# Weight loads of a mixed attention, convolution and scan kernel put on ScalarE's queue, and the fronts of its scan branches moved to other steps

## The chip, the cores and the metric

The kernel runs on one core of a Trainium2 chip. The metric is the device time of one launch in microseconds (us). Before the change it is 6692.09 us, the median of three executions that lie between 6676.76 and 6695.76 us. The profile shown here is of one further execution, with a span of 6680.2 us.

## The reference, cut to what matters

The input is a batch of 8 images of 256 channels and 32x32 pixels (1024 tokens), in float32. Four residual layers follow each other; each adds to `x` a function of the group-normalised `x`:

```
x = x + L0(gn(x))   # attention with 8 heads of 64, q and k normalised by length
x = x + L1(gn(x))   # 3x3 convolution 256 -> 256
x = x + L2(gn(x))   # 3x3 convolution 256 -> 256
x = x + L3(gn(x))   # layer norm, 4 Mamba branches (64 channels each, state of 16),
                    # gates, 1-d convolutions, a second attention, layer norms, 3x3 depthwise
```

A Mamba branch projects its 64 channels to 128, applies a short convolution and a gate, makes a step size `dt` and the vectors `B` and `C`, and runs along the 1024 tokens the recurrence `h = exp(dt*A)*h + dt*u*B`, `y = C.h`, for each of 128x16 states.

## The kernel before, in words

**Two streams side by side.** While the scans of image b run (`scan_layers`, L1019), the dense work of its neighbours runs beside them (`dense`, L1488): the last part of layer 3 of image b-1 (`back_layers`, L1184), the first attention of image b+1 (`front_attention`, L595), and then the two convolutions of image b+1 (`front_convs`, L769) mixed with the end of image b-1 (`back_end`, L1366). `interleave` (L1438) writes the two streams into one program: each dense piece yields a cost, and a step of the scans is put in whenever the costs have added up to `PACE` (2.95 for the middle images). So the six middle images repeat the same pattern.

**The order of instructions.** The framework lays the program out ahead of the run: each engine gets a fixed list, mostly in the order in which the pieces were written, and a buffer is given out again when its last reader is done. On the chip an engine works through its own list in order and waits at any entry whose inputs or buffer are not ready. Transfers are entries of such a list too: those written `nc.sync.dma_start` stand in SyncE's list (SP in the profile), those written `nc.scalar.dma_start` would stand in ScalarE's, between its activations. Before the change all 3328 transfers of the normal path stand in SyncE's list.

**The weights.** Small weights are loaded once. The large ones go through `chunk` (L150): it takes one of six buffers of the pool `wsp` (L45), loads a piece of 128 to 256 KB, and the matmuls right after it use it. The trace has 392 such loads (L156), 49 an image: 24 of them are the pieces of the two 3x3 convolutions (`in_wc1`, `in_wc2`; 192 KB, 12 matmuls written in the kernel as 3 taps x 2 halves with two passes each in the trace), the others are for the projections (`wqk`, `wv`, `wout`, `ainqk`, `ainv`, `rpw`, `fpw`, `fcw`, `projw`).

**The other transfers.** A scan unit is a quarter of the states of one half of the tokens, in two groups; there are 64 units an image, 16 a branch. `load` (inside `scan_steps`, L904) fetches two units ahead: `bc` (L937) every second unit, `dt` and `du` (L927) at the start of each half. Each is four transfers, into pools of two or three buffers. `store` (L795, its transfers at L799) writes `dt` and `du` of a branch to DRAM, L846 the rows of B and C.

**A unit on the engines.** GpSimd multiplies du by B (L950), ScalarE makes the decays `da` (an exp into PSUM), VectorE runs the scan over `hs`, GpSimd multiplies by C (L982), TensorE adds up over the states into `y`.

**The fronts.** What a branch needs before its first unit is made by `branch_front` (L803), a generator in six pieces: 0 the input projection into `raw`; 1 the short convolution `u` (one activation, three multiply-adds on VectorE, a tanh, one more multiply-add); 2 the projection `low` of u with `w_mxpw` and the storing of B and C; 3 dt before its softplus; 4 the softplus and the storing of dt; 5 du and its storing. `fronts` (L1040) says at which count n of scan steps each next piece is due (n is two more than the unit whose decays are being made). The tile `u` has two buffers (L818), so branch i takes over that of branch i-2, which `branch_back` (L876) reads for the last time in its second piece, two steps after the last unit's `y`.

In the profile nearly all engine work has line L102, the line of a helper (`Paced`) that records every operation, so the groups are told apart by their tiles: `big<-im,w` is a 3x3 convolution, `big<-local,w` the first half of the `fcw` projection, `da<-u,w_mxpw` piece 2 of a front.

Of the kernel before, what the change touches and what calls it, by code (L numbers as in the profile page):

```python
# [33 lines left out]
def preact_stack(ctx: ExitStack, tc: tile.TileContext, I, out, cols):  # L34
# [3 lines left out]
    nc = tc.nc  # L38
# [37 lines left out]
    def mwork(name):  # L76
        return mp.tile([P, N], F32, tag="m", name=name)

    def xm_tile(name):
        return xmp.tile([P, TP], F32, tag="xm", name=name)  # L80
# [69 lines left out]
    def chunk(name, i):  # L150

        src = fc_w if name == "fcw" else I[name]
        k, n = src.shape[2:]
        t = wsp.tile([P, HALF], F32, tag="w", name="w")
        t = t[:, 0 : k * n].rearrange("p (k n) -> p k n", n=n)
        nc.sync.dma_start(out=t, in_=src[i])  # L156
        return t

    minw = resident("minw")
# [23 lines left out]
    for base, sign in ((0, 1), (7, -1)):  # L183
        nc.gpsimd.affine_select(
            out=gmat,
            in_=gmat,
# [84 lines left out]
    def group_stats(mv, psum):  # L271

        with urgent():
            pg = psum()
            tensor.matmul(
                pg[:, 0:4], gmat, mv.rearrange("p a b -> p (a b)"), start=True, stop=True
            )
            g = sp.tile([P, 2, 2], F32, tag="g", name="g", bufs=4)
            vector.tensor_copy(g.rearrange("p a b -> p (a b)"), pg[:, 0:4])
            d = sp.tile([P, 2], F32, tag="d", name="d")  # L280
            vector.tensor_sub(d, mv[:, :, 0], g[:, :, 0])
            vector.tensor_mul(d, d, d)
            pd = psum()
            tensor.matmul(pd[:, 0:2], gmat, d, start=True, stop=True)
            rs = sp.tile([P, 2], F32, tag="rs", name="rs", bufs=4)
            vector.scalar_tensor_tensor(
                rs, pd[:, 0:2], 1e-5, g[:, :, 1], ALU.add, ALU.add
            )
            inverse_root(rs)
            shift = sp.tile([P, 2], F32, tag="shift", name="shift", bufs=4)  # L290
            vector.scalar_tensor_tensor(
                shift, g[:, :, 0], -1.0, rs, ALU.mult, ALU.mult
            )
        return rs, shift

    def group_norm(xt, stats, dsts, view=lambda a: a):
        with urgent():
            scale, shift = stats
            for t in range(2):
                scalar.activation(  # L300
                    dsts[t],
                    view(xt[:, t]),
                    AF.Identity,
                    bias=shift[:, t : t + 1],
                    scale=scale[:, t : t + 1],
                )
# [59 lines left out]
    def affine(wname, bname, func=AF.Identity):  # L366
        def finish(t, part):
            scalar.activation(
                part, part, func, bias=col(bname, t), scale=col(wname, t)
            )  # L370

        return finish

    def zero_ends(t):
        vector.memset(t[:, 0:1], 0.0)
        vector.memset(t[:, N + 1 : N + 2], 0.0)

    def inner(t):
        return t[:, 1 : N + 1]
# [11 lines left out]
    def project(name, srcs, evac):  # L391

        last = len(srcs) - 1
        for m in range(2):
            w = chunk(name, m)
            ps = big_tile()
            for k, src in enumerate(srcs):
                for h in range(2):
                    tensor.matmul(
                        ps[:, HALVES[h]],  # L400
                        w[:, k],
                        src[:, HALVES[h]],
                        start=k == 0,
                        stop=k == last,
                    )
            evac(m, ps)
            yield 2 * len(srcs) * 0.86

    def project_both(name, srcs, evac):

        last = len(srcs) - 1
        w = [chunk(name, m) for m in range(2)]
        ps = [big_tile() for _ in range(2)]
        for k, src in enumerate(srcs):
            for m in range(2):
                for h in range(2):
                    tensor.matmul(
                        ps[m][:, HALVES[h]],
                        w[m][:, k],
                        src[:, HALVES[h]],  # L420
                        start=k == 0,
                        stop=k == last,
                    )
                if k == last:
                    evac(m, ps[m])
            yield 4 * 0.86
# [168 lines left out]
    def front_attention(src, img, exact=False):  # L595
# [8 lines left out]

        v = vp.tile([P, NKT, 512], F32, tag="v", name="v")
        wv = [chunk("wv", c)[:, 0] for c in range(2)]
        for kt in range(0, NKT, 2):
            ps = big_tile()
# [267 lines left out]
    def branch_back(i, xn, br):  # L876

        j, rows = i // 2, slice((i % 2) * 64, (i % 2) * 64 + 64)
        u, z = br["u"], mwork("z")
        for h in range(2):  # L880
            ps = da_tile()
            tensor.matmul(
                ps,
                minw[rows, j, P : 2 * P],
                inner(xn[j])[rows, HALVES[h]],
                start=True,
                stop=True,
            )
            zh = z[:, HALVES[h]]
            scalar.activation(zh, ps, AF.Tanh, scale=0.5)  # L890
            vector.scalar_tensor_tensor(zh, zh, 1.0, ps, ALU.add, ALU.mult)
        vector.tensor_mul(u[:, 0:N], u[:, 0:N], z[:, 0:N])
        yield
        for h in range(2):
            ps = da_tile()
            tensor.matmul(
                ps[rows], moutw[:, i], u[:, HALVES[h]], start=True, stop=True
            )
            part = inner(xn[j])[rows, HALVES[h]]
            vector.scalar_tensor_tensor(  # L900
                part, part, half_skip[rows], ps[rows], ALU.mult, ALU.add
            )
# [116 lines left out]
    def scan_layers(img):  # L1019


        xt = img.pop("x")
        img["stats"] = group_stats(img.pop("mv"), da_tile)
        xn = [xm_tile("xn0"), xm_tile("xn1")]
        for t in xn:
            zero_ends(t)
        group_norm(xt, img["stats"], [inner(t) for t in xn])
        img["xd"] = xdp.tile([P, 2, N], F32, tag="xd", name="xd")
        nc.sync.dma_start(out=img["xd"], in_=xt)
        sq = [mwork("ln_sq"), mwork("ln_sq")]  # L1030
        yield
        yield from layer_norm(
            [inner(t) for t in xn], sq, BY_HALF, da_tile, affine("norm_w", "norm_b")
        )
        yield
        branches = [{} for _ in range(NB)]
        for _ in branch_front(0, xn, branches[0]):
            yield

        def fronts():  # L1040
            for i in range(1, NB):
                for n, _ in enumerate(branch_front(i, xn, branches[i])):
                    yield 16 * i - 10 + 7 * n // 4

        front, ending, due, n = fronts(), iter(()), 0, 0
        steps = scan_steps(branches)
        while True:
            next(ending, None)
            while due is not None and n >= due:
                due = next(front, None)  # L1050
            if next(steps, END) is END:
                break
            yield
            done = next(steps)
            if done is not None:
                ending = branch_back(done, xn, branches[done])
            n += 1
            yield
        yield from ending
        img["xm"] = xn  # L1060
# [471 lines left out]
    with tc.If(again > 0):  # L1532
        with tc.For_i(0, batch, 1) as i:
            img = {}
            src = x_in[bass.ds(i, 1)].rearrange("o (t p) n -> p (o t) n", p=P)
# [113 lines left out]
```

## Time and profile before

| | busy us | share of the span | instructions |
|---|---|---|---|
| TensorE (PE) | 5489.3 | 82% | 17310 |
| VectorE (DVE) | 4001.5 | 60% | 4612 |
| GpSimd (POOL) | 2723.7 | 41% | 1302 |
| ScalarE (ACT) | 2721.9 | 41% | 3253 |
| 16 DMA engines, SyncE's queue | | 24.6% | 216408 packets |

The granted TensorE clock is 0.891 of full speed in the mean. A middle image takes 799 us (for instance 1575 to 2374 us), with TensorE busy in 673.9 of them, VectorE in 508.9, ScalarE in 340.1 and GpSimd in 341.2.

How to read it: the share of an engine says little where the stages differ, so the reading goes by waits. A line of waits names the engine that waited and the tile it was to write, then what came last before it went on, then the total, the number of waits and the longest. `SPq` is SyncE's queue: time there is a transfer that stood at the head of the list and could not be issued yet. `PEld` is the loading of weights into TensorE, which overlaps the matmuls.

### The profile page before, as it was taken

To read this page: it belongs to the slowest core of one execution; us is meant where nothing else is said; L and a number is where in the kernel's file an instruction comes from. 1 tells how busy PE (TensorE), PEld (TensorE's weight loads), DVE (VectorE), ACT (ScalarE), POOL (GpSimd) and SP (SyncE) were. 2 spreads that over 40 slices of the span, in tenths; PEclk is the share of its full clock that TensorE was granted. 3 is DMA by queue.
4 is the path that set the end of the run, shared out by engine and by line. 5 is a ranking of instruction groups with operands and counts; after the bars stand their busy time and mean duration, and the time that the engine had idled before them with its cause. 6 is when DMAs were issued, how large, how long until landed. Compare 5 with 4: busy or idle time off the path is not lost.

```text
span 6680.2 us, 52240 instructions
## 1 busy us (share of the span) xinstructions
PE 5489.3 (82%) x17310; PEld 1854.4 (28%) x17310; DVE 4001.5 (60%) x4612; ACT 2721.9 (41%) x3253; POOL 2723.7 (41%) x1302
## 2 busy tenths in 40 slices
PE   8887688896988968888698886899788896877596
PEld 2331133222322223222242222322233222321232
DVE  4247744677555775467755667557765577555532
ACT  3234424553245523544335442354424553345332
POOL 0016662534435243542526435253352534456600
PEclk9988798998989989999899998999889897988697
DMA  1022232212223122321222212232122312233300
GB/s 50 27 60 79 74 92 73 83 58 68 86 74 91 42 76 71 94 81 44 79 82 77 78 50 78 73 88 70 54 86 72 91 51 73 77 93 84 90 20 30
DMA packets 216690, 470.83 MB, mean 70 GB/s; under 512 B 60116, under 2 KB 101716, under 8 KB 214360
## 3 DMA queue, kind: packets, MB, share of 16 engines
q1 hardware_dynamic: 216408, 467.38, 24.6%
q8 instruction: 139, 2.28, 0.1%
q14 instruction: 143, 1.17, 0.1%
HBM read 394.31 MB, written 64.49 MB: 69 GB/s over the span
## 4 chain that ended last, share of the span: by engine, by line
PE 55%; DVE 25%; issue 6%; DMA 5%; ACT 5%; POOL 3%; SPq 1%; DVEq 0%; POOLq 0%; ACTq 0%
PE big L102 36%; PE acc L102 11%; DVE p L102 6%; DVE hs L102 6%; PE da L102 5%; PE y L102 3%; DVE u L102 2%; POOL hs L982 2%; DVE t L102 2%; POOL hs L950 2%; DVE dw L102 1%; DVE dt L102 1%; DMA dt<-dt_m 1%; DVE y L102 1%; DVE st L102 1%
## 5 line engine op out<-in xcount | busy, mean ns | idle before, releaser
L950 POOL TENSOR_TENSOR hs<-du,bc 128x1024 f32<-128x1024 f32 x512 | 1310.7, 2573 | 1537.3 <-DMA dt<-dt_m 1182.9
L982 POOL TENSOR_TENSOR hs<-hs,bc 128x1024 f32<-128x1024 f32 x512 | 1327.0, 2592 | 1013.3 <-DVE hs L102 951.0
L102 PE MATMUL big<-im,w 128*128 128x512 f32 x2304 | 1096.9, 630 | 338.5 <-DMA w<-in_wc 253.1
L102 ACT ACTIVATE p<-big 128x1024 f32<-128x1024 f32 x1024 | 1039.5, 1021 | 799.1 <-PE big L102 795.3
L102 PE MATMUL acc<-p,v 128*64 128x512 f32 x4096 | 1167.4, 640 | 0.7 <-ACT o L102 0.7
L102 ACT ACTIVATE da<-dt,a_neg 128x512 f32<-128x512 f32 x1024 | 687.7, 687 | 1004.7 <-DVE hs L102 711.6
L102 DVE TENSOR_TENSOR p<-p 128x1024 f32<-128x1024 f32 x448 | 777.0, 1734 | 271.4 <-ACT p L102 183.3
L102 DVE TENSOR_TENSOR_SCAN hs<-da,hs 128x512 f32<-128x512 f32 x512 | 603.0, 1210 | 477.4 <-ACT da L102 250.6
L102 DVE TENSOR_TENSOR_SCAN hs<-da,carry,hs 128x512 f32<-128x512 f32 x512 | 624.9, 1266 | 256.9 <-POOL hs L950 133.9
L102 PE MATMUL big<-qk,qk 64*128 64x512 f32 x2048 | 655.0, 674 | 105.9 <-ACT p L102 94.1
L102 PEld LDWEIGHTS big<-im,w 128*128 128x128 f32 x2304 | 447.7, 200 | 999.1 <-issue 870.3
L102 PE MATMUL big<-q,k 64*128 64x512 f32 x2048 | 604.8, 661 | 79.1 <-ACT big L102 39.6
L981 POOL COPY carry<-hs 128x2 f32<-128x2 f32 x256 | 95.8, 374 | 1089.8 <-DVE hs L102 1060.3
L102 PE MATMUL y<-hs,sel 128*32 128x512 f32 x2048 | 408.8, 723 | 153.7 <-POOL hs L982 153.5
L102 PEld LDWEIGHTS acc<-p,v 128*64 128x64 f32 x4096 | 214.1, 138 | 827.9 <-issue 732.3
L102 PEld LDWEIGHTS big<-qk,qk 64*128 64x128 f32 x2048 | 178.0, 195 | 570.9 <-issue 298.3
L102 PEld LDWEIGHTS big<-q,k 64*128 64x128 f32 x2048 | 162.8, 191 | 509.9 <-issue 274.6
L102 DVE SCALAR_TENSOR_TENSOR dw<-xo,vec,dw 128x992 f32<-128x992 f32 (+1 forms) x128 | 227.4, 1824 | 27.3 <-ACT dw L102 26.7
L102 PE MATMUL big<-xn,w 128*128 128x512 f32 x512 | 232.6, 608 | 6.7 <-ACT p L102 6.7
L102 DVE SCALAR_TENSOR_TENSOR xt<-big,vec,xt 128x1024 f32<-128x1024 f32 x48 | 61.4, 1280 | 226.9 <-PE big L102 226.9
L102 PE MATMUL big<-o,w 128*128 128x512 f32 x384 | 179.0, 615 | 15.9 <-DVE o L102 15.9
L102 DVE SCALAR_TENSOR_TENSOR u<-raw,vec,u 128x1024 f32<-128x1024 f32 x96 | 150.1, 1564 | 64.4 <-ACT u L102 63.9
(210 smaller groups left out, 4987.2 us busy)
## 6 DMA issues: line engine op xcount, KB each, us to landing
bc<-bc SPq DMA_DIRECT2D x1024, 128.0 KB
dt<-dt_m SPq DMA_DIRECT2D x512, 128.0 KB
du<-du_m SPq DMA_DIRECT2D x512, 128.0 KB
w<-in_wc SPq DMA_DIRECT2D x192, 192.0 KB
rs<-inv SPq DMA_DIRECT2D x64, 256.0 KB
dt_m<-dt SPq DMA_DIRECT2D x64, 256.0 KB
du_m<-a SPq DMA_DIRECT2D x64, 256.0 KB
xt<-in_x SPq DMA_DIRECT2D x8, 1024.0 KB
```

What stands on the lines that cost most here:

```text
L102: made = issue(*args, **kwargs)
L950: nc.gpsimd.tensor_mul(u["hs"], u["du"], both_groups(u["bc"][:, 0]))
L981: nc.gpsimd.tensor_copy(carry[:, u["q"], g : g + 2], hs[:, :, HALF - 1])
L982: nc.gpsimd.tensor_mul(hs, hs, both_groups(u["bc"][:, 1]))
```

## The change

Two edits. The loads of the weights that stay only for their use are issued from ScalarE's list in place of SyncE's. And the pieces of the fronts of branches 1 to 3 become due at other steps: the offsets from 16*i were -10, -9, -7, -5, -3, -2 and become -12, -10, -8, -6, -3, -1. The value yielded after piece k is when piece k+1 is due; that after the last piece is when piece 0 of the next branch is due. So pieces 1 to 5 of branch 1 move from n = 6, 7, 9, 11, 13 to 4, 6, 8, 10, 13, and piece 0 of branch 2 from 14 to 15.

What it is for: the weights no longer stand in one list with the transfers of the scans, and the pieces of a front lie further apart.

```diff
@@ def chunk(name, i):
         t = wsp.tile([P, HALF], F32, tag="w", name="w")
         t = t[:, 0 : k * n].rearrange("p (k n) -> p k n", n=n)
-        nc.sync.dma_start(out=t, in_=src[i])
+        nc.scalar.dma_start(out=t, in_=src[i])
         return t
@@ def scan_layers(img):
         def fronts():
             for i in range(1, NB):
                 for n, _ in enumerate(branch_front(i, xn, branches[i])):
-                    yield 16 * i - 10 + 7 * n // 4
+                    yield 16 * i - 12 + 9 * n // 4
```

## The prediction

> **What bounds the kernel now.** I read the page first, then who waited for whom, then the waits of SyncE's own queue, then the timeline of the longest wait.
>
> The chain that ended last is mostly TensorE:
>
> ```profile
> PE 55%; DVE 25%; issue 6%; DMA 5%; ACT 5%; POOL 3%; SPq 1%; DVEq 0%; POOLq 0%; ACTq 0%
> ```
>
> TensorE is busy for 5489 of 6680 us, so a time saved must come from its 1191 us of idling or shorten something it waits for. Three of its waits concern the edits:
>
> ```profile
> PE big L102 <- DMA w<-in_wc: 253.1, 8, 40.3
> ...
> PE da L102 <- DVE u L102: 80.7, 16, 8.8
> ...
> PE big L102 <- DMA w<-fc_w: 65.1, 7, 10.1
> ```
>
> The first is the prize: a convolution stands for a weight piece eight times, six of them for 39 to 40 us, once in each middle image; the other two (image 1) are 17.4 us together. Bandwidth is not why: the DMA engines are 24.6% busy. SyncE's queue, which has all transfers in one list, shows why:
>
> ```profile
> SPq L156 <- PE big L102: 1132.6, 216, 34.1
> SPq L937 <- POOL hs L982: 928.1, 130, 34.0
> ...
> SPq L927 <- ACT da L102: 504.1, 89, 21.4
> SPq L927 <- POOL hs L950: 456.8, 79, 15.2
> ```
>
> Weights (L156) stand there until TensorE frees one of six buffers, and the scans' loads (L937, L927) until the scan frees theirs. Either holds up the other. The timelines of SyncE and of TensorE in one such case (start, length, instruction, count):
>
> ```profile
> 1560.27 2.05 SPq L156 DMA_DIRECT2D w<-in_wc  x2
> 1571.11 1.73 SPq L927 DMA_DIRECT2D du<-du_m  x4
> ...
> 1638.44 1.70 SPq L927 DMA_DIRECT2D du<-du_m  x4
> 1640.18 0.88 SPq L937 DMA_DIRECT2D bc<-bc  x2
> 1651.97 11.66 SPq L927 DMA_DIRECT2D dt<-dt_m  x8
> 1663.74 1.75 SPq L927 DMA_DIRECT2D du<-du_m  x4
> 1665.59 0.37 SPq L156 DMA_DIRECT2D w<-in_wc  x1
> ```
> ```profile
> 1627.44 2.84 PE L102 MATMUL big<-im,w 128*128 128x512 f32 x6
> 1669.36 2.90 PE L102 MATMUL big<-im,w 128*128 128x512 f32 x3 [39.08 <-DMA w<-in_wc]
> ```
>
> From 1562 to 1665 us no weight is issued, while the convolution uses up its six buffers (1575 to 1630). The first of the six was free again at about 1585, when its twelve matmuls were over; the next pieces stood behind du, dt and bc of the next half, which waited for the scan. The three matmuls after the gap take 0.97 us each in place of 0.45.
>
> **What the Trainium skill says.** "DMA: Bandwidth & Descriptors", section "Anatomy of one DMA — SWDGE (gpsimd) path", says that DMA engines do not wait on semaphores: any wait happens on the issuing sequencer before dispatch. The rows of SyncE's queue agree (1132.6 us at L156). The same page, section "Issuing engines are not separate DMA queues", says that issuing from several engines only saves the sequencer's issue time, since all run on the same 16 DMA engines. So the edit buys no bandwidth; what this trace adds is that it also takes a wait at the head of one list away from the other.
>
> **The change, part by part.**
>
> *Convolution weights.* On ScalarE a piece stands between activations and can go when its buffer is free. ScalarE is busy for 9.5 us of the 39, so it gets to it long before 1665. I take the wait as gone. What comes in its place? The busy times over the stages of these convolutions:
>
> ```profile
> core 0: us, PE busy (x) PEld busy (x) DVE busy (x) ACT busy (x) POOL busy (x), PEclk, DMA share, GB/s
> ...
> 1575.00:1630.00 55.00, 51.63 (x152) 21.97 (x152) 36.41 (x44) 25.68 (x29) 29.78 (x15) 0.88 0.24 72
> 1630.00:1669.00 39.00, 0.29 (x1) 0.00 (x0) 35.16 (x33) 9.48 (x11) 17.57 (x7) 0.57 0.28 73
> 1669.00:1713.00 44.00, 40.87 (x104) 15.51 (x104) 32.39 (x25) 5.93 (x9) 30.98 (x15) 0.95 0.34 93
> 1713.00:1840.00 127.00, 112.49 (x344) 50.84 (x344) 70.65 (x113) 42.36 (x51) 49.71 (x25) 0.91 0.26 82
> ```
>
> VectorE works through the gap (35.2 of 39 us: scans and depthwise convolution) and takes the convolution's result out. If all its work of 1630 to 1713 (35.2 + 32.4 = 67.6 us) must still come before the second convolution, these 83 us shrink by only 15. If it can slide into the second convolution, where VectorE has 127 - 71 = 56 us free, all 39 are saved. I take the middle, 27 us an image.
>
> *The fc weights.* 65.1 us in seven waits, about 10 an image. The matmuls they release are followed by others on `o`, whose factors `rs` are loaded at the same time, so I count half: 5 us.
>
> *The other weights* made no wait worth naming, so moving them gains nothing; TensorE's earlier work hides them.
>
> *The fronts.* Pieces 1 and 2 of branch 1 were one step apart (n = 6, 7); now two (4, 6). In the middle images TensorE waits 8.7 us for u in the first of these places and 3.1 us in the second (11.9 an image), with the matmuls of the attention queued behind `da<-u`. A step is 7 to 12 us there (a scan unit begins every 7 to 12 us around 1940 us), so one more step could hide it; the matmul may also just be taken up sooner and wait the same. Half: 6 us. For branches 2 and 3, piece 1 is now due at n = 16i-12, in the step where branch i-2's `u` is still to be read; it waits for that buffer for about one step and then has lost its lead. No gain, no loss: the pieces after it are due a step earlier or at the same step. dt is stored a step sooner; its loads waited for dt's storing rarely (dt rows of ScalarE's waits: 61.6 us in the whole run), so nothing.
>
> *What ScalarE pays.* An issue on SyncE takes 0.36 us (median of the 192 convolution loads; 0.33 to 0.42). The skill gives about 0.05 us for dispatch in the same section "Anatomy of one DMA"; the trace decides. 49 x 0.36 = 17.6 us an image. And it adds a wait: ScalarE may reach a convolution's piece before TensorE has freed the buffer. Behind it in ScalarE's list stand the decays of the scan, for which VectorE waits, and in the attention the exps, for which TensorE waits. The trace cannot show it; the bounds are 0 and one piece of matmuls (12 in 5.35 us) for each of 24 pieces, 128 us. I take 1 us each, 24 us, since ScalarE mostly waits for VectorE and for TensorE itself there and so comes late. Of ScalarE's time few us count: it has 5% of the chain at 41% busy, one in eight. (17.6 + 24)/8 = 5 us an image.
>
> *Sum.* A middle image gains 27 + 5 + 6 - 5 = 33 us; six make 198. Image 1 with its 17.4 us of waits gains about 12, the first and last nothing. 6692 - 210 = 6482 us.
>
> **The rivals.**
> (a) *VectorE becomes the bound.* For it: 35 of 39 us busy in the gap. Then the convolution gains 10, fc 5, the fronts 0, ScalarE costs 5: 10 us x 6 = 60, so 6632 us. Against it: 56 us free in the next stage.
> (b) *All of it is recovered.* 39 + 10 + 12 - 2 = 59 us x 6 + 25 = 379: 6313 us. For it: the matmuls after a gap also run slower, which ends. Against: VectorE, as above.
> (c) *Slower: the wait moves to ScalarE.* If it meets each piece early it stands up to 128 + 18 = 146 us an image, and the decays and exps behind it stand too; if a third of it is on the path, 48 us, against 38 gained: ten us an image over eight, 80 us slower, 6772 us. For it: 216 waits at L156 for TensorE now, and the transfers share completion semaphores (rows of SyncE's waits where a load stands for an unrelated transfer, as L937, bc, for du_m<-a, 26.3 us), so ScalarE could also come to wait for SyncE's transfers. Against it: ScalarE is idle for 460 of 799 us.
> (d) *No change:* the scan sets the pace through the `y` matmuls, 6690 us.
>
> **How the numbers follow.** The forecast 0.50, (a) 0.22, (b) 0.09, (c) 0.13, (d) 0.06. The forecast is that of the likeliest, 6482. The range reaches from near (b), 6340, where about 0.07 lies below, to 6710, which takes in (a) and (d) and leaves out most of (c), about 0.12. Faster by over 0.3% (below 6672): 0.50 + 0.22 + 0.09 = 0.81; same 0.06; slower 0.13.
>
> **What would show it.** Right: `PE big <- DMA w<-in_wc` falls from 253 us to under 30 and `w<-fc_w` from 65 to under 35, a middle image takes about 766 us, TensorE's busy time stays near 5480, the rows of SyncE's queue at L156 are gone. Fronts: the 8.7 us wait for u falls. Rival (a): VectorE over 90% busy through both convolutions, TensorE's evacuations waiting for it. Rival (c): `ACT` rows that end with `PE big` at the place of the loads, longer waits of `DVE hs` for `ACT da` (372.9 us now) and of `PE big` for `ACT p` (128.1 now). I would be wrong if the pieces stood as late in ScalarE's list as in SyncE's, behind decays that wait for the scan: then TensorE's 39 us would stay.

## The result, and the profile after

The changed kernel takes 6536.18 us (median; 6529.43 to 6541.66) beside 6685.99 us for the kernel before in the same comparison (6676.76 to 6695.76). The ratio is 0.9775, with a 95% interval from 0.9756 to 0.9795: faster by 150 us. The forecast was 6482 us, a gain of 210.

Who waited for whom in the changed kernel (engine and tile, what it waited for: total us, times, longest us):

```profile
ACT da L102 <- PE big L102: 299.3, 42, 10.2
...
DVE hs L102 <- ACT da L102: 275.8, 128, 11.1
PE y L102 <- POOL hs L982: 267.9, 101, 16.0
...
PE big L102 <- ACT p L102: 180.4, 56, 13.5
...
PE da L102 <- DVE u L102: 10.0, 2, 8.4
```

The waits of TensorE for `w<-in_wc` (253.1 us before) and for `w<-fc_w` (65.1) have no row any more, and that for `u` fell from 80.7 to 10.0. In their place stand other rows: `PE y` for GpSimd grew from 153.5 to 267.9 us, `PE big` for `p` from 128.1 to 180.4. With the weights moved alone the first of these is 254.9 and the second 119.9; with the fronts moved alone they are 173.3 and 170.5, so the one comes with the weights and the other with the fronts. The row at the top is new: ScalarE waits for TensorE where its next entry is a piece of weights whose buffer is in use. What it delays most, the decays that VectorE waits for, is waited for less than before (275.8 in place of 372.9).

SyncE's queue in the changed kernel:

```profile
...
SPq L937 <- POOL hs L982: 623.8, 100, 26.6
...
SPq L927 <- POOL hs L950: 490.8, 65, 17.6
...
SPq L937 <- DMA w<-in_wc: 258.6, 39, 9.7
```

L156 is gone. The last row is a surprise: loads of `bc` on SyncE wait until a weight that ScalarE issued has landed. The weights now go out between activations (ScalarE's timeline in a middle image: start, length, instruction, count):

```profile
2336.13 0.33 ACTq L156 DMA_DIRECT2D w<-in_wc  x1
2336.51 0.69 ACT L102 ACTIVATE da<-dt,a_neg 128x512 f32<-128x512 f32 x1 [4.90 <-DVE raw L102]
...
2351.09 0.33 ACTq L156 DMA_DIRECT2D w<-in_wc  x1
...
2360.11 0.33 ACTq L156 DMA_DIRECT2D w<-in_wc  x1
...
2371.65 0.33 ACTq L156 DMA_DIRECT2D w<-in_wc  x1
```

One piece every 5 to 12 us here, where SyncE had issued none for 103 us in the passage that the prediction shows. But the convolution gave back a good part of the 39 us. Here are the busy times of the first convolution of the fourth image, and of its second with what follows, up to the first matmul of the attention's stage (`big<-rd,w`): of before, and then of after (stretch, length, then busy us of PE, PEld, DVE, ACT, POOL; TensorE clock, DMA share, GB/s):

```profile
2374.10:2521.90 147.80, 95.44 (x268) 38.29 (x268) 110.89 (x116) 42.16 (x50) 82.93 (x38) 0.80 0.29 80
2521.90:2639.10 117.20, 109.52 (x333) 49.86 (x333) 63.75 (x97) 41.45 (x50) 45.06 (x23) 0.94 0.25 81
```
```profile
2328.90:2455.70 126.80, 97.73 (x259) 38.61 (x257) 103.39 (x112) 39.41 (x47) 65.61 (x30) 0.85 0.28 80
2455.70:2578.10 122.40, 111.16 (x339) 49.57 (x337) 64.42 (x99) 40.23 (x49) 57.27 (x30) 0.95 0.29 90
```

The first stretch is 21.0 us shorter and the second 5.2 longer. VectorE is 82% busy in the first, from 75%. TensorE's own waits in that first stretch, before and after, show what came in place of the 39 us:

```profile
PE big L102 <- DMA w<-in_wc: 39.1, 1, 39.1
PE big L102 <- ACT im L102: 4.6, 1, 4.6
PE y L102 <- POOL hs L982: 3.3, 3, 1.2
...
```
```profile
PE y L102 <- POOL hs L982: 18.6, 7, 8.6
PE da L102 <- DVE t L102: 6.0, 1, 6.0
...
```

TensorE now waits for the scans' products themselves, seven times, and for VectorE. With the smaller rows its waits there fell from 50.5 us to 29.1; without the 39.1 alone they would have been 11.4.

To find the rest I cut each trace at the matmuls of stages that occur once an image: the two convolutions (`big<-im,w`), the tail between the end of the second and the first `big<-rd,w` (the start of `back_layers` and of the next scans), the stage of the attention from `big<-rd,w` to `big<-local,w`, and the rest up to the next convolution. The columns are the stages of the passage that begins with the third image's first convolution, in us, and the span of the scans that start in it. "Weights" stands for the new queue, "fronts" for the new steps.

| kernel | conv 1 | conv 2 | tail | attention | rest | image | its scans |
|---|---|---|---|---|---|---|---|
| before | 147.9 | 94.9 | 22.4 | 294.6 | 239.1 | 798.9 | 692.8 |
| after | 126.6 | 97.8 | 24.9 | 278.0 | 240.4 | 767.7 | 659.1 |
| weights alone | 132.8 | 97.9 | 25.1 | 289.6 | 240.3 | 785.6 | 680.5 |
| fronts alone | 141.6 | 95.3 | 25.7 | 278.6 | 240.5 | 781.6 | 672.5 |

And the whole span of each profiled run, cut at the first `big<-rd,w` of images 0, 6 and 7 (counted from 0, so image 1 is the second), as differences from before:

| kernel | start (1041.0) | six middle images (4793.3) | last scans (554.8) | end (291.0) |
|---|---|---|---|---|
| after | +1.3 | -174.6 | +34.8 | -1.8 |
| weights alone | +7.7 | -88.4 | +30.9 | -1.7 |
| fronts alone | -9.4 | -120.0 | +13.9 | -1.3 |

So a middle image gained 29.1 us (174.6/6; forecast 33), and the scans of the last image lost 34.8 us, which no step of the prediction had.

### The profile page after: what moved, and what is told of

Its sections match the earlier page's. It is cut to its first block, busy times and chain, and to the rows that moved or that the text cites. A ratio compares the mean times of both kernels' runs of the same rounds, so it can differ in the third digit from the quotient of the medians.

```text
span 6539.9 us, 52206 instructions
## 1 busy us (share of the span) xinstructions
PE 5511.5 (84%) x17310; PEld 1859.0 (28%) x17310; DVE 4006.1 (61%) x4612; ACT 2718.8 (42%) x3253; POOL 2704.5 (41%) x1302
## 5 line engine op out<-in xcount | busy, mean ns | idle before, releaser
L982 POOL TENSOR_TENSOR hs<-hs,bc 128x1024 f32<-128x1024 f32 x512 | 1311.3, 2562 | 952.2 <-DVE hs L102 860.5
L102 PE MATMUL acc<-p,v 128*64 128x512 f32 x4096 | 1153.3, 637 | 3.1 <-ACT p L102 1.3
L102 DVE TENSOR_TENSOR p<-p 128x1024 f32<-128x1024 f32 x448 | 766.1, 1710 | 312.1 <-ACT p L102 180.4
L102 PE MATMUL big<-qk,qk 64*128 64x512 f32 x2048 | 641.0, 671 | 142.2 <-ACT p L102 130.3
L102 PE MATMUL y<-hs,sel 128*32 128x512 f32 x2048 | 442.1, 687 | 268.0 <-POOL hs L982 267.9
L102 DVE SCALAR_TENSOR_TENSOR dw<-xo,vec,dw 128x961 f32<-128x961 f32 (+1 forms) x128 | 239.3, 1914 | 29.9 <-ACT dw L102 29.2
L102 PEld LDWEIGHTS y<-hs,sel 128*32 128x32 f32 x2048 | 58.4, 113 | 559.6 <-POOL hs L982 408.9
L102 ACT ACTIVATE big<-big 128x1024 f32<-128x1024 f32 x64 | 64.5, 1008 | 276.7 <-DVE q L102 222.2
```

Source lines behind the costliest of these rows:

```text
L102: made = issue(*args, **kwargs)
L982: nc.gpsimd.tensor_mul(hs, hs, both_groups(u["bc"][:, 1]))
```

## The experiments

**Which part brings what.** First the two parts apart. Weights on ScalarE, fronts as before:

```diff
-                    yield 16 * i - 12 + 9 * n // 4
+                    yield 16 * i - 10 + 7 * n // 4
```

> Weights on ScalarE's list, fronts at their old steps. Theory (the weights' edit carries most of the gain: the convolution's wait of 39 us an image goes, about half of it comes back as time, and fc's wait goes too): 6575 to 6605 us, wait of PE big for w<-in_wc under 30 us, the 8.7 us wait of da<-u for u stays. Rival (the fronts carry it, the weights' wait is only handed on to the scans): 6650 us or more although the wait is gone.

Measured: 6630.47 us, ratio 0.9914 (0.9897 to 0.9931). Both are missed: the wait is gone, and only 54 us with it, where the theory had 80 to 110. Then the fronts alone, the weights on SyncE's list:

```diff
-        nc.scalar.dma_start(out=t, in_=src[i])
+        nc.sync.dma_start(out=t, in_=src[i])
```

> Weights on SyncE's list, fronts at the new steps. Theory: the 39 us wait an image stays, the waits for u (8.7 and 3.1 us in a middle image) go: 6640 to 6670 us. Rival (the fronts carry it): 6600 us or less. If the 33 us that the last image lost come from the fronts, the stretch of the last scans is longer here than in the kernel before, and not so in the run with the old fronts.

Measured: 6574.55 us, ratio 0.9838 (0.9823 to 0.9852). The rival is right: the fronts, for which I had counted 6 us an image, bring 110 us, twice what the weights do. The waits of this kernel:

```profile
PE big L102 <- DMA w<-in_wc: 251.5, 8, 40.2
...
PE da L102 <- DVE u L102: 10.5, 4, 8.4
...
PE big L102 <- DMA w<-fc_w: 5.7, 1, 5.7
```

The weights of the convolution are waited for as before, but the fc weights hardly at all, though they still stand in SyncE's list. Either edit removes that wait.

**Which weights.** Only the two 3x3 convolutions' pieces on ScalarE, new fronts:

```diff
-        nc.scalar.dma_start(out=t, in_=src[i])
+        queue = nc.scalar if name in ("wc1", "wc2") else nc.sync
+        queue.dma_start(out=t, in_=src[i])
```

> The changed kernel, but only the weights of the two 3x3 convolutions on ScalarE's list, all others back on SyncE's. Theory: only the waits for the fc weights come back (about 10 us in each of seven images, half on the path): 6555 to 6580 us. Rival (the other weights on ScalarE hold up the exps of the attention): faster than the changed kernel, under 6520 us.

Measured: 6542.9 us, ratio 0.9789 (0.9776 to 0.9802), nearer to even than I had thought, and not for the reason given: here the third image's passage takes 774.6 us, 7 more than after (the second convolution 104.8 in place of 97.8), and the last scans 565.2, 24 less than after. The 7 us are a wait: in the second convolution of each of the six middle images TensorE waits 6.2 or 6.3 us for `w<-in_wc` once (37.6 in all), a row that the kernel after does not have. So the other weights do gain something in the middle on ScalarE, and lose it at the end. Why a piece of the convolution comes late when they stay on SyncE was not tested.

**What ScalarE pays.** Every load in two halves, so 392 issues more:

```diff
-        nc.scalar.dma_start(out=t, in_=src[i])
+        for rows in (slice(0, 64), slice(64, P)):
+            nc.scalar.dma_start(out=t[rows], in_=src[i][rows])
```

> The changed kernel with each weight loaded in two transfers of 64 partitions: 392 more issues on ScalarE of 0.33 us each (131 us more of it), same bytes. Theory (ScalarE has room, one us in eight counts): 6536 + 16, between 6536 and 6570 us. Rival (ScalarE's list is on the path for much of the time): half or more of the 131 us, 6600 us or more.

Measured: 6551.63 us, ratio 0.9802 (0.9788 to 0.9816). At the 0.334 us that an issue takes on ScalarE (median of the changed kernel), 392 more are 131 us of its time; some 15 us of them show, about one in eight. (Each of the two medians stands for executions that lie up to 12 us apart, so the 15 are rough.)

**Was the wait one for VectorE?** Four of the eight outer taps of the depthwise convolution (`dw`) are left out, so that VectorE has about 15 us less in the first convolution (8 of 1.82 us). The same edit was made to the kernel before and to the kernel after:

```diff
             for n, k in enumerate((0, 1, 2, 3, 5, 6, 7, 8)):
+                if n < 4:
+                    if n % 2:
+                        yield 1
+                    continue
```

> The kernel before with four of the eight outer taps of the 3x3 depthwise convolution left out (eight multiply-adds of VectorE an image, about 1.9 us each, 15 us; the output is then not the reference's). Theory (the 39 us wait for weights is only handed on: SyncE's list waits for the scan, the scan for VectorE): the wait shrinks by 8 us or more in each of six images, and 15 us go in the tail: 6570 to 6620 us. Rival (the wait comes from the order of the list whatever VectorE does): the wait stays at 39 us, only the tail gains, 6650 us or more.

> The changed kernel with the same taps left out. Theory (with the list's wait gone, VectorE sets the two convolution stages): 8 us or more an image go from them, and 15 us in the tail: 6425 to 6475 us. Rival (TensorE or the weights set them): only the tail gains, 6510 us or more.

Measured: 6616.48 us on before (ratio 0.9891, 0.9874 to 0.9908) and 6469.09 on after (0.9674, 0.9658 to 0.9689), both within what was expected, though all that is gained lies in the first convolution and nothing more in what follows. The waits of TensorE in the first of the two:

```profile
PE big L102 <- DMA w<-in_wc: 188.1, 8, 29.1
```

With VectorE's work cut and no transfer touched, the longest wait for a weight falls from 40.3 to 29.1 us, and the first convolution from 147.9 to 136.5. The wait was put down to a DMA, but the 11 us of it that went were VectorE's time. That it was handed on through the scan, the buffers of `du` and `bc`, and SyncE's list is read from that list's rows, not tested step by step. In the kernel after, where that wait is gone, the same cut still shortens the first convolution by 9.8 us (126.6 to 116.8): VectorE's work still sets a part of its length.

**The last scans.** In the last turn of the loop over the images (the scans of the last image beside the end of the one before it) and in what follows, all weights go back to SyncE, the rest as after:

```diff
+    late = [False]
@@ chunk
-        nc.scalar.dma_start(out=t, in_=src[i])
+        queue = nc.sync if late[0] else nc.scalar
+        queue.dma_start(out=t, in_=src[i])
@@ for b in range(batch):
+        late[0] = b == batch - 1
```

> The changed kernel, but in the last iteration (the scans of image 7 beside the end of image 6) and the tail the weights are issued by SyncE again. Theory (there the scans set the end, and weights that come sooner only let dense work of VectorE and TensorE in ahead of them): the 24 to 31 us that the last iteration lost come back, 6500 to 6520 us. Rival (the loss there comes from the fronts): 6530 us or more.

Measured: 6509.65 us, ratio 0.9739 (0.9724 to 0.9753). Then the last image's fronts are put back as well:

```diff
-                    yield 16 * i - 12 + 9 * n // 4
+                    yield 16 * i - 10 + 7 * n // 4 if late[0] else 16 * i - 12 + 9 * n // 4
```

> As the run before this one, and the fronts of the last image at their old steps too. Theory (the fronts cost the last iteration some 14 us, as in the run with the new fronts alone): 6485 to 6508 us. Rival (no further gain, the two losses are one): the same as the run before this one.

Measured: 6503.13 us, ratio 0.9723 (0.9709 to 0.9737), the fastest kernel of this study that does all the work: 33 us less than after, 26.5 of them from the weights and 6.5 from the fronts, for which some 14 were expected. In the profiled runs the stretch "last scans" of the table above falls from 589.6 us after to 566.1 and then to 554.3 (before: 554.8). Here it is cut into the attention that runs beside these scans and what follows, for before, after, and this kernel:

```profile
5834.00:6238.00 404.00, 303.44 (x897) 79.33 (x898) 217.20 (x207) 186.76 (x231) 244.14 (x124) 0.83 0.33 89
6238.00:6389.00 151.00, 86.65 (x248) 39.35 (x246) 97.25 (x122) 48.45 (x57) 80.04 (x37) 0.70 0.24 68
```
```profile
5661.00:6040.00 379.00, 299.83 (x872) 79.10 (x872) 203.23 (x189) 175.26 (x215) 216.68 (x110) 0.82 0.33 87
6040.00:6251.00 211.00, 103.31 (x275) 42.48 (x274) 134.11 (x138) 59.34 (x72) 108.23 (x50) 0.66 0.23 63
```
```profile
5661.00:6064.00 403.00, 302.90 (x897) 78.85 (x897) 217.06 (x207) 186.11 (x230) 243.57 (x123) 0.83 0.33 89
6064.00:6216.00 152.00, 87.73 (x249) 40.11 (x250) 97.96 (x122) 49.19 (x57) 80.90 (x38) 0.69 0.23 69
```

After the change the attention is 25 us shorter there, but GpSimd (fifth busy time) did 27 us less of the scans in it, and the stretch behind it is 60 us longer. In the kernels before and after, `big<-rd,w` of the last image begins 27 us after the end of its scans, so here the scans set the end, and they took 504 us in place of 470. That the weights on ScalarE cause most of it is shown by the two runs; that it is because the dense work, with its weights there sooner, took turns from the scans is argued, not shown.

**Why do the fronts bring so much?** The prediction's reason was the distance of pieces 1 and 2. Four more ways to set the steps follow, the first two with the weights on ScalarE, the others with the weights on SyncE. Sooner by two, not spread:

```diff
-                    yield 16 * i - 12 + 9 * n // 4
+                    yield 16 * i - 12 + 7 * n // 4
```

> The changed kernel with the fronts begun two steps sooner but not spread (offsets -12, -11, -9, -7, -5, -4: pieces 1 and 2 one step apart again). Theory (the fronts' 20 us an image come from the room between pieces 1 and 2, so that TensorE no longer waits for u): the wait of da<-u for u comes back and costs 8 to 12 us an image, 6585 to 6615 us. Rival (it is having dt and du in DRAM sooner): 6520 to 6550 us.

Measured: 6531.47 us, ratio 0.9762 (0.9745 to 0.9778). TensorE waits for `u` again:

```profile
PE da L102 <- DVE u L102: 72.4, 16, 9.6
```

That is 7.7 us in a middle image (11.9 before), and yet the whole gain is kept, so the spacing falls as the reason. The gain lies elsewhere, though: in the third image's passage the attention takes 270.9 us here and the second convolution with its tail 137.1, where after has 278.0 and 122.6. Spread, not sooner:

```diff
-                    yield 16 * i - 12 + 9 * n // 4
+                    yield 16 * i - 10 + 9 * n // 4
```

> The changed kernel with the fronts spread out but not begun sooner (offsets -10, -8, -6, -4, -1, +1: du is stored one step before its first load). Theory: the wait for u stays away and most of the gain is kept, but the scans may wait for du at the start of a branch, 6530 to 6580 us. Rival (sooner is what counts): 6590 us or more.

Measured: 6630.22 us, ratio 0.9913 (0.9897 to 0.993). The wait for `u` is gone (1.6 us), and so is the fronts' gain: the weights alone took 6630.47. (This kernel also has its last pieces later than before, so it does not price the spread by itself.) Then piece 1 alone two steps sooner, all else as before:

```diff
-                    yield 16 * i - 10 + 7 * n // 4
+                    yield 16 * i - 10 + 7 * n // 4 - 2 * (n == 0)
```

> The kernel before (weights on SyncE) with one offset changed: piece 1 of branches 1 to 3 two steps sooner (-12 in place of -10), the rest as it was. Theory: the waits for u go, the attention beside the scans gets 9 to 16 us an image shorter, 6580 to 6630 us. Rival (all pieces matter, the wait for u was hidden anyway): 6665 us or more.

Measured: 6607.12 us, ratio 0.9876 (0.986 to 0.9893): some 80 us of the fronts' 110 come from starting piece 1 sooner. (This also puts pieces 1 and 2 three steps apart in place of one; the two runs above say that the distance is not what brings the gain. Pieces 4 and 5, which store dt and du, keep their steps here, so having these sooner is not what brings the 80.) Last, for which branch? The new steps for branch 1 only, all else as before:

```diff
-                    yield 16 * i - 10 + 7 * n // 4
+                    yield 16 * i - 12 + 9 * n // 4 if i == 1 else 16 * i - 10 + 7 * n // 4
```

> The kernel before (all weights on SyncE's list) with the new steps for the front of branch 1 alone; branches 2 and 3 keep the old ones. The new steps for all three had given 6574.55 us, 112 less than before. The prediction's step: branch 1 carries what the fronts bring, branches 2 and 3 nothing since their first piece waits for the buffer of u; then this kernel has nearly all of it, 6565 to 6595 us, and the stage of the attention (end of the second convolution's tail to the next image's projection) is about 279 us in a middle image, as with all three moved. The rival: the sooner start counts for each branch; then one of three is worth about a third, 6630 to 6665 us, with the stage at 285 us or more. In between, both carry.

Measured: 6649.39 us, ratio 0.9957 (0.9943 to 0.9971). The rival is right: branch 1 brings 30 us, so by difference some 80 come with branches 2 and 3, for which the prediction had counted nothing. One row of the waits seems to go with this: VectorE waiting in piece 1 for ScalarE's first step of `u`. It was 63.9 us before, 64.1 with the spread alone, and in the kernels for branch 1 only and with all fronts moved:

```profile
DVE u L102 <- ACT u L102: 58.2, 15, 5.2
```
```profile
DVE u L102 <- ACT u L102: 8.2, 11, 3.2
```

It is 7.9 us with piece 1 alone sooner and with the fronts sooner by two. But the kernel with halved loads, whose fronts are sooner too, has 110.5 us in this row, nearly all of it in branch 1's piece (17 us in each middle image), and lost only some 15 us. So the row does not price the gain. ScalarE's timeline for the front of branch 2 in the fourth image, of before and of the fronts alone (it is made beside the units of branch 1, the first of which begins at 2833.5 and 2778.5 us):

```profile
2867.32 1.02 ACT L102 ACTIVATE p<-big 128x1024 f32<-128x1024 f32 x1 [1.33 <-PE big L102]
2868.24 1.23 ACT L102 ACTIVATE u<-raw,vec 128x1024 f32<-128x1024 f32 x1
```
```profile
2800.63 1.24 ACT L102 ACTIVATE u<-raw,vec 128x1024 f32<-128x1024 f32 x1
```

Before, `u` starts 34.7 us after that begin, behind the attention's exps, and VectorE waits 5.5 us for it. With the new steps it starts 22.1 us after it, as soon as the buffer is free: the last matmul that reads the old `u` (`da<-u,w_moutw`) ends at 2800.59 us. The projection of `u` moves from 47.1 to 42.9 us after the begin. For branch 3, beside the units of branch 2, `u` moves from 85.1 to 60.3 us and its projection from 105.8 to 87.3.

## Why the prediction was right or wrong

The total is right within its range, but two of its terms were wrong in opposite directions, and one loss was missing.

*The convolution weights: mechanism right, size wrong.* Two streams in one list held each other up; with the weights in another list the wait is gone, and bandwidth had no part in it. The step that failed is "I take the middle, 27". The two ends had been 15 and 39, and a new wait stands where the old one was: TensorE waits 18.6 us for the scans' products in place of 3.3. The whole term with fc and ScalarE's cost (27 + 5 - 5) measured 14.7 us a middle image alone (88.4/6) and 9.1 on top of the fronts (29.1 - 20.0). In the third image's passage of the kernel with the weights alone the first convolution shrank by 15.1, the lower end, which was VectorE's work; the second and the tail grew by 5.7. The reason for the middle, VectorE's 56 free us in the next stage, was a count of idle time, and idle time there did not take up enough of the work. VectorE's busy time in the second stretch hardly grew (63.8 to 64.4 us). The runs with fewer taps show that VectorE was behind part of the wait. Rival (a) had the size right (10 us of the convolution's 39), but not what it named as its mark: VectorE is 82% busy in the first convolution and 53% in the second, not over 90. Rival (d) named the wait that came in, that for the scans through `y`, but the scans' pace left room for a gain.

*The fc weights: 5 us counted.* The wait went, but with either edit, so it belongs to neither alone. That is one reason why the two parts (14.7 and 20.0 us a middle image) bring 29.1 together and not 34.7.

*The other weights: "moving them gains nothing".* In the middle images wrong by some 6 us (29.1 against 23.0, from 138.1/6, with only the convolutions' moved); given back at both ends of the run, so nothing in the total.

*The fronts: 6 us counted, 20.0 measured alone, 14.4 on top of the weights.* The wait for `u` in the third image's attention did go, all 11.9 us of it where I took half (3.1 of them stand in branch 2's front, for which the same paragraph counts nothing), but the sooner fronts without the spread show that this wait is not what the gain hangs on. The step that failed is the one on branches 2 and 3: that piece 1 "waits for that buffer for about one step and then has lost its lead. No gain, no loss". It does wait for the buffer, but `u` keeps 12.6 us of lead in branch 2 (34.7 - 22.1) and 24.8 in branch 3 (85.1 - 60.3), and about 80 of the 110 us come with these branches. In the third image's attention with the fronts alone, TensorE's waits for `u` (11.9 us) and for `w<-fc_w` (9.9) are gone, and those for `p` are longer (14.3 to 20.8). Mean times of the 16 scan units of each branch, images 1 to 6 (begin of one branch's units to begin of the next):

| kernel | branch 0 | branch 1 | branch 2 | branch 3 |
|---|---|---|---|---|
| before | 128.4 | 200.8 | 237.4 | 125.0 |
| branch 1's front moved | 118.5 | 203.7 | 238.5 | 125.1 |
| all fronts moved | 118.5 | 192.8 | 234.6 | 125.3 |
| after | 119.4 | 193.2 | 235.0 | 113.2 |

Each front that moves shortens the units beside which it is made, against the row above it: by 10 us, 11 and 4. Part of the 11 may be the fc wait, which falls among the units of branch 1: the weights alone make these 193.6 us. On top of the fronts, the weights take 12 off the last branch, which runs beside the end of the first convolution and the second. What passes a sooner `u` on to the units of the branch before it stays open: VectorE's wait for ScalarE in piece 1 is 9 us an image less (55.7/6), but the kernel with halved loads has longer waits of this kind, in branch 1's piece, without losing the gain, and each of these edits also gives the engines' lists another order.

*ScalarE pays: 5 us counted.* The issues' share was right: one in eight of 131 us forecasts 16, and 15 were measured. The waits were underestimated as waits: the new row of ScalarE behind TensorE is 299 us, some 46 in a middle image, in place of my 24. But with halved loads it is 78.7 and with the fronts sooner only 192.3, and the times do not follow it, so it lies mostly off the path. Rival (c) falls.

*Image 1 "gains about 12, the first and last nothing".* Image 1 gained nothing at the start (+1.3): its first convolution fell from 117.3 to 101.9 and its second grew from 73.5 to 90.7. The last scans lost 34.8 us, and the scans of a last image that set the end there were not looked at. The sum as measured: +1.3 - 174.6 + 34.8 - 1.8 = -140.3 us in the profiled runs; the prediction's 198 + 12 + 0.

*What would show it.* The rows came as said: no wait for `w<-in_wc` or `w<-fc_w`, L156 off SyncE, 767.7 us for the third image's passage (766 forecast; 769.8 in the mean of the six), TensorE busy for 5511.5 us (near 5480). These signs could not tell whether the terms behind them were right; only the two parts run apart did. That the total came within 54 us of 6482 is in part luck: the weights' term was too high, the fronts' too low and its reason wrong, and a loss was left out.

## What to carry to other kernels

A long wait for a load behind a mixed list can be removed by another issuing engine, but ask first what the head of that list waits for: what the head's releaser has to do remains, and here the gain (15.1 us in the first convolution) was the lower bound that this work sets, not the wait of 39. Starting a front that is made beside a pipeline as soon as its buffer allows brought more here than removing the wait did, so a lead of a dozen microseconds is worth measuring rather than being argued away. And look at the last round by itself: where the other stream sets the end, give back there what helps the dense work.

## What the runs showed of the hardware that was not expected

A transfer issued by one engine can hold up the list of another: SyncE waits 258.6 us at L937 for landings of weights that ScalarE issued, in 39 waits of at most 9.7 us. The semaphores on which transfers report their landing are shared: each of the eight in this trace serves transfers of both engines. The prediction named this as a risk for ScalarE; SyncE bears most of it.

The granted clock was higher where there were fewer gaps, and that is a second, smaller gain. In the fourth image's attention with the fronts alone, 833 matmuls keep TensorE busy for 246.9 us at a clock of 0.94, where before as many took 253.5 at 0.91: 6.7 of the 16 us saved there, the rest being idle time (41.1 to 31.7 us). The Trainium skill, "TensorE: Matmul & The Clock Gate", section "Part 1: The HAM clock gate (the "warmup" mystery)", says that the clock is set by how busy TensorE has been of late; these rows agree in direction; no run here shows more of it.

The skill's rule that several issuing engines only save issue time ("DMA: Bandwidth & Descriptors", section "Rules for kernel authors") is too narrow for this kernel: 49 issues of about 0.35 us are 17 us of SyncE's time an image, and what vanished was a wait of 39 us at TensorE, though less than half of that came out as time (14.7 us a middle image with the weights alone).
